# A Restormer block on one core: the depthwise conv of every fourth channel chunk on TensorE in 5 of 12 middle bands instead of 3 of 7, with the whole instruction order computed anew

## The chip, the cores and the metric

The kernel runs on one core of a Trainium2 chip. The metric is device time in microseconds (us). The engines are TensorE (PE, with its weight loads as PEld), VectorE (DVE), ScalarE (ACT), GpSimd (POOL) and SyncE (SP, which only issues DMAs here). The time before is 4030.19 us, the median of three runs.

## The reference

The input is 16 images of 128 channels by 96 by 96 pixels, all in float32. Each image goes through a block of two parts:

```python
xn1 = layernorm(x over channels)
q, k, v = xn1 @ wq.T, xn1 @ wk.T, xn1 @ wv.T       # 8 heads of 16 channels
attn = softmax((q / |q|) @ (k / |k|).T * 16**-0.5)  # 16 x 16 for each head, over all pixels
x = x + (attn @ v) @ wp.T
xn2 = layernorm(x over channels)
h1 = w_in @ xn2                                     # 128 -> 512 channels
h2 = depthwise 3x3 conv of h1, zero padding          # 9 taps for each channel
x = x + w_out @ gelu(h2)                            # 512 -> 128 channels
```

The attention is over channels, so one image's attention needs a sum over all its pixels before any pixel can go on. The feed-forward part is local to a pixel, but for the 3x3 conv.

## The kernel before

**Tiles.** An image is cut into 6 bands of 16 rows (`BR`), a band into 4 units of 4 rows (`UR`, 384 pixels). Over all images there are 96 bands, numbered g. The 512 hidden channels are 4 chunks n of 128. Normalised pixels lie in a ring of rows (`xn`), from which TensorE reads.

**Two ways to do a conv.** For chunks 0, 1 and 2 of each band, and for chunk 3 of some, the conv is a *job* (`conv_job`). TensorE computes the hidden rows (`hidden`, L952), 16 to 18 of them in three or four matmuls; a float32 matmul stands in the trace as two instructions. ScalarE moves each to SBUF with its bias (`kept`, L955). VectorE does six of the nine taps, plus the centre, as six `scalar_tensor_tensor` instructions on 16 rows (`tap`, L982): the first reads 1536 elements per partition, the others 1520, or 1425 where the outer tap row lies outside the image. For the other two taps ScalarE writes the product (`product`, L975) and GpSimd issues DMAs that add one product to the other and the sum to the result (`add_products`, L989: one is "add_last", one is "add_first"). ScalarE copies two rows to the top of the buffer for the next band (`halo`, L947) and applies gelu (L993).

For chunk 3 of the other bands (`by_matmuls`), TensorE does everything: each tap's diagonal is multiplied into the weights beforehand (`comp`), so that nine products accumulate in PSUM for each unit (L1047), and ScalarE applies gelu with the right bias at the image's edges (L1062, three instructions a unit, six where the unit touches the top or the bottom). There is no DVE tap, no product, no added DMA and no halo in that way.

Which bands go the second way is decided by `by_pe(g)`:

```python
k = NG - 1 - g
if g < NB:
    return g in PE_FIRST
return k in PE_LAST if k < NB else (k + 1) * PE_SHARE[0] // PE_SHARE[1] > k * PE_SHARE[0] // PE_SHARE[1]
```

The first image (bands 1, 3, 5) and the last (`PE_LAST`, four bands) have lists of their own; `PE_SHARE` holds for the 84 bands between.

**After the conv.** `ffn_out` multiplies the four chunks with `woutT` (L1082, eight instructions a unit), ScalarE copies the result (`evicted`, L1092), and a DMA issued by GpSimd adds a band to the output in DRAM (`add_out`, L1096), to which SP has stored the attention's result (`store_x2`). In the last two bands VectorE adds (L1089) and SP stores.

**Around it.** Each image has two norm passes: transposes to pixels (L694), statistics on VectorE (L701), the power on GpSimd (L712), scaling on ScalarE (L737), for the first pass the gram matrix (L746), transposes back (L780) and a copy into the ring (L783). The attention between them is a chain of small steps on all engines. `mix` (L643) applies it, ScalarE moves the result (`mixed`, L652), and a DMA issued by GpSimd adds the input (`add_x`, L655).

**The order.** Every step is put on record as an operation with an engine, a duration, a due place counted in jobs, and what it reads and writes. `Plan.order` plays all of them through once, when the kernel is built: an engine that is free takes the ready operation with the lowest place, if a buffer is free, and the operations are written out in the order of their starts. On the chip each engine then runs its own list in this order. A place is the job's number plus an offset from `AT`, with separate offsets (names ending in `_0`) for the first image; `SLACK` adds to how long a result is held back for other engines, and `add` and `move` set the durations of DMAs issued by GpSimd and SP:

```python
def add(p, f, r, w, n=BR, dram=False):
    late = T_DRAM if dram else (0, 0.01)
    op("POOL", 800, p, f, r, w, 350 + SLACK["ADD"], late[1], (T_ADD[0] + n * (T_ADD[1] + late[0])) * 108 / 100)
```

There are 15 buffers for results and products of the conv (`h3`), 4 PSUM banks shared by `hidden`, `by_matmuls`, `ffn_out` and `mix`, and two PSUM buffers for the transposes to pixels.

Of the kernel before, what the change touches and what calls it, by code (L numbers as in the profile page):

```python
# [19 lines left out]
XR = 8  # L20
RING = 124
PE_CHUNK = 3
PE_SHARE = [3, 7]
PE_LAST = (0, 1, 3, 4)
PE_FIRST = [1, 3, 5]
HEAD = 2
# [10 lines left out]
LAST_ADDS = 2  # L37
IN_TURN = ("tr", "xb", "x1")
AT = dict(
    load_1=-98.0, load_2=97.25, tables=85.15, weights=-792.45, zeros=79.7, load_a=-138.9, forth_a=-4.35,  # L40
    stats_a=-21.2, variance_a=-32.7, power_a=-106.65, scaled_a=-54.6, gram=7.8, back_a=-40.4, place_a=-40.15,
    attention=-134.7, mix=-2.85, residual=-281.65, mixed=-12.35, add_x=85.8, forth_b=-9.45, stats_b=-42.85,
    variance_b=31.9, power_b=-14.4, shift_b=-138.5, scaled_b=-461.4, back_b=-7.75, place_b=288.55, evicted=90.4,
    add_out=52.9, halo=120.1, hidden=4.7, kept=-885.75, products=643.55, add_last=35.65, tap=248.3,
    add_first=70.15, gelu=273.2, conv=3.75, conv_gelu=-926.85, out=8.15, add=-117.65, store=67.75, mix_0=-49.95,
    residual_0=-107.3, mixed_0=-51.7, add_x_0=25.0, gram_0=363.7, forth_a_0=-122.3, forth_b_0=-8.35,
    stats_a_0=6.3, stats_b_0=31.35, scaled_a_0=-127.55, scaled_b_0=120.9, back_a_0=-24.7, back_b_0=-58.05,
    place_a_0=-41.75, place_b_0=-85.55, shift_b_0=-22.25, late=69.2, store_x2=-58.9, store_x2_0=-116.55,
    variance_a_0=-270.4, variance_b_0=-83.0, power_a_0=-136.0, power_b_0=76.85, attention_0=-297.05,
    load_a_0=-428.55, hidden_0=2.8, kept_0=126.55, products_0=350.15, tap_0=79.7, add_last_0=-519.2,  # L50
    add_first_0=-230.95, gelu_0=18.6, conv_0=2.5, conv_gelu_0=113.55, out_0=6.35, evicted_0=-10.75,
)
STEP = dict(scaled=0.3, hidden=0.1, products=0.5, tap=0.166, conv=1.6, conv_tap=0.03, out=0.8, out_part=0.05)
SLACK = dict(PE=450, DVE=120, ACT=130, POOL=400, ADD=420, MOVE=290)
NORM1_END = 6.0
EARLY = 5
WAIT = dict(POOL=1130, SP=1470, ACT=1470)
# [4 lines left out]
T_ADD, T_DRAM, T_MOVE = (65, 227), (15, 750), 125  # L62


class Plan:
# [15 lines left out]
    def op(self, engine, ns, place, work, reads, writes, result, own=None, dma=0, two=False):  # L81

        k = len(self.ops)
        needs = {}
        for t in reads:
            if t in self.writer:  # L90
                needs[self.writer[t]] = True
        for t in writes:
            if t in self.writer:
                needs[self.writer[t]] = True
            for r in self.readers.get(t, ()):
                needs[r] = True
        for t in reads:
            self.readers.setdefault(t, []).append(k)
        new = []
        for t in writes:  # L100
            self.writer[t], self.readers[t] = k, []
            if t[0] in self.free and t[:2] not in self.users and t[:2] not in new:
                new.append(t[:2])
        for t in {t[:2]: None for t in (*reads, *writes)}:
            if t[0] in self.free:
                self.users.setdefault(t, []).append(k)
                needs[self.users[t][0]] = True
        needs.pop(k, None)
        self.ops.append((engine, ns, place, work, list(needs), new, result, own or result, dma, two))
# [129 lines left out]
def tile_restormer_block(  # L239
# [138 lines left out]
    op = plan.op  # L378
# [27 lines left out]
    def pe(ns, p, f, r, w):  # L406
        op("PE", ns, p, f, r, w, ns + 200 + SLACK["PE"], ns)

    def dve(ns, p, f, r, w, two=False):
        op("DVE", ns, p, f, r, w, ns + 120 + SLACK["DVE"], ns + 125, two=two)  # L410

    def pool(ns, p, f, r, w):
        op("POOL", ns, p, f, r, w, ns + 33 + SLACK["POOL"])

    def add(p, f, r, w, n=BR, dram=False):
        late = T_DRAM if dram else (0, 0.01)
        op("POOL", 800, p, f, r, w, 350 + SLACK["ADD"], late[1], (T_ADD[0] + n * (T_ADD[1] + late[0])) * 108 / 100)

    def move(p, f, r, w, n=XR):
        op("SP", 430, p, f, r, w, 350 + SLACK["MOVE"], dma=n * T_MOVE)  # L420

    def act(ns, p, f, r, w):
        op("ACT", ns, p, f, r, w, ns + 150 + SLACK["ACT"], ns + 144)

# [202 lines left out]
    def norm(i, second, place_of):  # L627
# [8 lines left out]
        def x2(s, u):  # L636
# [35 lines left out]
            if u % UPX == UPX - 1:  # L672
                add(at("add_x", s, i), add_x, [], whole, XR, True)
# [257 lines left out]
    def conv_job(j, g, n):  # L931
# [82 lines left out]
        for k, t in enumerate(dma_taps[1:]):  # L1014
            add(at("add_last", j, g >= HEAD), lambda t=t: add_products(t), [pr[1 + k]], [pr[0]], rows_of(t))
# [3 lines left out]
        if dma_taps:  # L1019
            add(at("add_first", j, g >= HEAD), lambda: add_products(dma_taps[0]), [pr[0]], h3, rows_of(dma_taps[0]))  # L1020
# [103 lines left out]
    def by_pe(g):  # L1124
# [5 lines that stand above are left out]
# [57 lines left out]
```

## Time and profile before

| | |
|---|---|
| median of three runs | 4030.19 us (4029.83 to 4032.23) |
| the profiled execution's own time | 4030.8 us |
| its span, first to last instruction | 4029.1 us |
| granted TensorE clock, mean | 0.999 |
| PE busy | 3983.6 us (99%) |
| PEld busy | 2602.8 us (65%) |
| DVE busy | 3959.4 us (98%) |
| ACT busy | 3707.7 us (92%) |
| POOL busy | 1889.7 us (47%) |

A group's row reads: line, engine, operation, result and operands, count, then busy time in us and mean ns of one, then the engine's idle time just before these instructions. Busy time counts overlapping instructions of one engine once. In a table of windows each engine's entry is its busy us, with the number of instructions in brackets, and behind them stand the granted clock, the mean busy share of the 16 DMA engines and GB/s.

### The profile page before, as it was taken

The page shows a single profiled execution, that of the slowest core. Times are in us where ns is not written, and L with a number is a line of the kernel's source. Part 1 is how long each engine was busy: PE and PEld are TensorE (multiplying, and loading weights), DVE is VectorE, ACT ScalarE, POOL GpSimd, SP SyncE. Part 2 cuts the span into 40 slices and gives each one's busy share as a digit, 9 for nine tenths or more (in the row PEclk, how much of TensorE's full clock was granted, in tenths as well). Part 3 has the DMA queues.
Part 4 walks back from the last instruction along what each step waited for, and adds up shares of the span by engine and source line. Part 5 has one row for each costly group of instructions (what it writes and reads, how often), then busy time and mean ns, then how long its engine had stood idle before and what let it go on. Part 6 is the DMA issues. An engine that isn't in the chain of part 4 may idle for free. (4 is left out here: it accounts for less than half of the span.)

```text
span 4029.1 us, 51274 instructions
## 1 busy us (share of the span) xinstructions
PE 3983.6 (99%) x17112; PEld 2602.8 (65%) x17112; DVE 3959.4 (98%) x3472; ACT 3707.7 (92%) x7680; POOL 1889.7 (47%) x1594
## 2 busy tenths in 40 slices
PE   9999999999999999999999999999999999999999
PEld 7666666666666666656666666666666666666565
DVE  6999999999999999999999999999999999999998
ACT  7999999899999999989989899999989999999985
POOL 4544455454454544545455453544545544454431
PEclk9999999999999999999999999999999999999999
DMA  5999899999999999999999999999999999999987
GB/s 147 208 197 223 185 214 205 209 225 197 220 222 201 218 203 230 213 202 219 198 216 210 198 220 198 230 205 211 224 194 227 206 217 216 202 221 189 218 177 152
DMA packets 196872, 832.64 MB, mean 207 GB/s; under 512 B 22784, under 2 KB 24320, under 8 KB 196608
## 3 DMA queue, kind: packets, MB, share of 16 engines
q0 software_dynamic: 138672, 677.52, 85.6%
q1 hardware_dynamic: 57936, 151.83, 10.5%
q8 instruction: 137, 2.24, 0.2%
q14 instruction: 127, 1.04, 0.1%
HBM read 150.62 MB, written 149.42 MB: 74 GB/s over the span
## 5 line engine op out<-in xcount | busy, mean ns | idle before, releaser
L982 DVE SCALAR_TENSOR_TENSOR h<-h,ratio,h 128x1520 f32<-128x1520 f32 (+1 forms) x1707 | 2980.5, 1780 | 8.0
L1082 PE MATMUL h<-h,woutT 128*128 128x384 f32 x3072 | 1135.3, 489 | 8.0 <-ACT h L955 7.1
L1047 PE MATMUL h<-xn,comp 128*128 128x380 f32 (+3 forms) x3162 | 1097.7, 476 | 1.8 <-ACT h L955 0.9
L975 ACT ACTIVATE h<-h,ratio 128x1536 f32<-128x1536 f32 (+1 forms) x680 | 1088.7, 1610 | 4.8 <-PE h L1082 2.9
L952 PE MATMUL h<-xn,winT 128*128 128x384 f32 (+3 forms) x2712 | 1059.9, 494 | 5.2 <-ACT h L955 2.2
L989 POOL DMA_DIRECT2D h<-h x680 | 640.2, 968 | 892.2 <-ACT h L975 390.1
L955 ACT ACTIVATE h<-h,beta 128x384 f32<-128x384 f32 (+1 forms) x1314 | 794.1, 632 | 83.0 <-PE h L952 67.6
L1082 PEld LDWEIGHTS h<-h,woutT 128*128 128x128 f32 x3072 | 557.6, 191 | 347.3 <-issue 39.9
L1047 PEld LDWEIGHTS h<-xn,comp 128*128 128x128 f32 x3162 | 567.0, 190 | 312.9 <-issue 16.6
L712 POOL TENSOR_TENSOR rstd_a<-ve_a,mhalf 128x4 f32<-128x4 f32 x288 | 508.8, 1767 | 449.4 <-ACT ve_a L708 429.0
L712 POOL TENSOR_TENSOR rstd_b<-ve_b,mhalf 128x4 f32<-128x4 f32 x288 | 537.1, 1886 | 351.6 <-ACT ve_b L708 337.9
L952 PEld LDWEIGHTS h<-xn,winT 128*128 128x128 f32 x2712 | 485.6, 190 | 276.1 <-issue 21.8
L982 DVE SCALAR_TENSOR_TENSOR h<-h,ratio 128x1536 f32<-128x1536 f32 x341 | 617.7, 1812 | 2.5 <-ACT h L955 1.4
L993 ACT ACTIVATE h<-h 128x1536 f32<-128x1536 f32 (+1 forms) x344 | 520.1, 1514 | 8.4 <-DMA h<-h 4.5
L737 ACT ACTIVATE zT<-pT_b,rstd_b 128x128 f32<-128x128 f32 x1132 | 331.5, 409 | 21.9 <-POOL rstd_b L712 20.7
L737 ACT ACTIVATE zT<-pT_a,rstd_a 128x128 f32<-128x128 f32 x1080 | 318.1, 412 | 3.2 <-POOL rstd_a L712 1.6
L746 PEld LDWEIGHTS g<-zT 128*128 128x128 f32 x2160 | 275.3, 191 | 43.2 <-issue 0.4
L643 PE MATMUL h<-xn,mwT 128*128 128x384 f32 x768 | 296.3, 489 | 3.5 <-ACT h L1062 1.0
L655 POOL DMA_DIRECT2D x<-in_x_dram x189 | 179.2, 964 | 238.4 <-ACT x L652 161.8
L746 PE MATMUL g<-zT 128*128 128x129 f32 x2160 | 285.2, 274 | 0.0
L652 ACT ACTIVATE x<-h,d 128x384 f32<-128x384 f32 x378 | 225.8, 629 | 13.0 <-PE h L643 7.2
L1062 ACT ACTIVATE h<-h,edge 128x376 f32<-128x376 f32 (+2 forms) x558 | 162.6, 387 | 71.2 <-PE h L1047 70.5
(185 smaller groups left out, 3212.6 us busy)
## 6 DMA issues: line engine op xcount, KB each, us to landing
h<-h POOLq DMA_DIRECT2D x567, 768.0 KB, 10.0
h<-h POOLq DMA_DIRECT2D x113, 720.0 KB, 11.9
x<-in_x_dram SPq DMA_DIRECT2D x192, 384.0 KB, 7.8
out_dram<-x SPq DMA_DIRECT2D x190, 384.0 KB, 9.6
x<-in_x_dram POOLq DMA_DIRECT2D x189, 384.0 KB, 10.3
out_dram<-h POOLq DMA_DIRECT2D x94, 768.0 KB, 10.4
out_dram<-x SPq DMA_DIRECT2D x4, 192.0 KB, 1.9
h<-in_L_conv_w_in_dram SPq DMA_DIRECT2D x1, 256.0 KB, 2.8
```

Source lines behind the costliest of these rows:

```text
L643: nc.tensor.matmul(rows(pm), lhsT=mats[i][0], rhs=interior(i, u), start=True, stop=True)
L712: nc.gpsimd.tensor_tensor(rstd, d["ve"], mhalf, ALU.pow)
L737: nc.scalar.activation(zT(q)[:, k, :P], d["pT", q][:, k, :], AF.Copy, scale=d["rstd"][:, t : t + 1])
L746: nc.tensor.matmul(grams[i][:, : P + 1], lhsT=zt[:, :P], rhs=zt, start=(q == 0 and k == 0), stop=(q == NU * TPU // QT - 1 and k == QT - 1),)
L952: nc.tensor.matmul(rows(ph)[:, k : k + m, :], lhsT=winT[:, n, :], rhs=z, start=True, stop=True)
L955: nc.scalar.activation(window(h1_, r, e - r, 1), rows(d.pop(("ph", r))), AF.Identity, bias=beta[:, n : n + 1])
L975: nc.scalar.activation(d["pr", t][:, o0:o1, :], shifted(t, o0, o1), AF.Copy, scale=ratio[:, n, t : t + 1])
L982: nc.vector.scalar_tensor_tensor(h3[:, o0:o1, w0:w1], shifted(t, o0, o1, w0, w1), ratio[:, n, t : t + 1], onto, ALU.mult, ALU.add)
L989: nc.gpsimd.dma_start(out=to[:, o0:o1, :], in_=d["pr", t][:, o0:o1, :], accum_op=ALU.add)
L993: nc.scalar.activation(h3, h3, AF.Gelu)
L1047: nc.tensor.matmul(d["pc"][:, o0 + k : o0 + k + m, w0:w1], lhsT=comp[:, t, :], rhs=z[:, :, w0 + dx : w1 + dx], start=(t == order[0]), stop ...
L1082: nc.tensor.matmul(rows(d["po"]), lhsT=woutT[:, n, :], rhs=h3s[g, n][:, s * UR : (s + 1) * UR, :], start=(k == 0), stop=(k == NCH - 1),)
```

## The change

`PE_SHARE` becomes 5 of 12. Of the 84 bands of the 14 middle images 35 instead of 36 have their fourth chunk on TensorE, and they lie at other places: with 5 of 12 the pattern repeats every two images. The offsets of all due places, two slacks and the planner's costs of an accumulating DMA are other numbers too, and the order that follows from them is computed anew. No instruction's own code changes.

```diff
-PE_SHARE = [3, 7]
+PE_SHARE = [5, 12]
...
 AT = dict(
-    load_1=-98.0, load_2=97.25, tables=85.15, weights=-792.45, zeros=79.7, load_a=-138.9, forth_a=-4.35,
-    stats_a=-21.2, variance_a=-32.7, power_a=-106.65, scaled_a=-54.6, gram=7.8, back_a=-40.4, place_a=-40.15,
-    attention=-134.7, mix=-2.85, residual=-281.65, mixed=-12.35, add_x=85.8, forth_b=-9.45, stats_b=-42.85,
-    variance_b=31.9, power_b=-14.4, shift_b=-138.5, scaled_b=-461.4, back_b=-7.75, place_b=288.55, evicted=90.4,
-    add_out=52.9, halo=120.1, hidden=4.7, kept=-885.75, products=643.55, add_last=35.65, tap=248.3,
-    add_first=70.15, gelu=273.2, conv=3.75, conv_gelu=-926.85, out=8.15, add=-117.65, store=67.75, mix_0=-49.95,
...
+    load_1=67.95, load_2=66.0, tables=-10.25, weights=-1.25, zeros=102.0, load_a=-138.05, forth_a=-4.35,
+    stats_a=-71.15, variance_a=-7.95, power_a=-38.85, scaled_a=-26.15, gram=7.8, back_a=-19.55, place_a=-53.7,
+    attention=-132.65, mix=-2.85, residual=-143.35, mixed=-11.45, add_x=583.2, forth_b=-9.45, stats_b=-240.2,
+    variance_b=3.45, power_b=-0.35, shift_b=62.8, scaled_b=-128.9, back_b=-8.05, place_b=116.65, evicted=28.7,
+    add_out=137.25, halo=51.0, hidden=4.7, kept=-219.85, products=688.85, add_last=163.15, tap=38.55,
+    add_first=429.0, gelu=66.75, conv=3.75, conv_gelu=-117.0, out=8.15, add=-143.05, store=-82.3, mix_0=-98.55,
...
 )
-SLACK = dict(PE=450, DVE=120, ACT=130, POOL=400, ADD=420, MOVE=290)
+SLACK = dict(PE=440, DVE=120, ACT=130, POOL=400, ADD=420, MOVE=0)
...
-        op("POOL", 800, p, f, r, w, 350 + SLACK["ADD"], late[1], (T_ADD[0] + n * (T_ADD[1] + late[0])) * 108 / 100)
+        op("POOL", 1000, p, f, r, w, 350 + SLACK["ADD"], late[1], (T_ADD[0] + n * (T_ADD[1] + late[0])) * 107 / 100)
```

The offsets cut here include `store_x2` (-58.9 before, -176.25 after) and all those of the first image.

More of the change, by code (lines that the diff above doesn't have):

```diff
@@ L45 @@
-    add_first=70.15, gelu=273.2, conv=3.75, conv_gelu=-926.85, out=8.15, add=-117.65, store=67.75, mix_0=-49.95,
[L46 to L49, printed above, removed]
@@ L50 @@
-    load_a_0=-428.55, hidden_0=2.8, kept_0=126.55, products_0=350.15, tap_0=79.7, add_last_0=-519.2,
-    add_first_0=-230.95, gelu_0=18.6, conv_0=2.5, conv_gelu_0=113.55, out_0=6.35, evicted_0=-10.75,
+    load_1=67.95, load_2=66.0, tables=-10.25, weights=-1.25, zeros=102.0, load_a=-138.05, forth_a=-4.35,
+    stats_a=-71.15, variance_a=-7.95, power_a=-38.85, scaled_a=-26.15, gram=7.8, back_a=-19.55, place_a=-53.7,
+    attention=-132.65, mix=-2.85, residual=-143.35, mixed=-11.45, add_x=583.2, forth_b=-9.45, stats_b=-240.2,
@@ new lines @@
+    variance_b=3.45, power_b=-0.35, shift_b=62.8, scaled_b=-128.9, back_b=-8.05, place_b=116.65, evicted=28.7,
+    add_out=137.25, halo=51.0, hidden=4.7, kept=-219.85, products=688.85, add_last=163.15, tap=38.55,
+    add_first=429.0, gelu=66.75, conv=3.75, conv_gelu=-117.0, out=8.15, add=-143.05, store=-82.3, mix_0=-98.55,
+    residual_0=102.75, mixed_0=-53.0, add_x_0=-59.8, gram_0=147.5, forth_a_0=134.55, forth_b_0=-7.8,
+    stats_a_0=-37.7, stats_b_0=-37.4, scaled_a_0=76.85, scaled_b_0=46.25, back_a_0=147.9, back_b_0=-39.95,
@@ L52 @@
+    place_a_0=123.9, place_b_0=-117.0, shift_b_0=-120.65, late=153.0, store_x2=-176.25, store_x2_0=-117.5,
+    variance_a_0=75.05, variance_b_0=-414.1, power_a_0=-184.2, power_b_0=188.85, attention_0=-138.6,
+    load_a_0=-265.85, hidden_0=2.7, kept_0=2.25, products_0=120.45, tap_0=3.0, add_last_0=-99.45,
+    add_first_0=157.4, gelu_0=11.85, conv_0=2.4, conv_gelu_0=74.5, out_0=7.35, evicted_0=65.7,
 )
 STEP = dict(scaled=0.3, hidden=0.1, products=0.5, tap=0.166, conv=1.6, conv_tap=0.03, out=0.8, out_part=0.05)
-SLACK = dict(PE=450, DVE=120, ACT=130, POOL=400, ADD=420, MOVE=290)
+SLACK = dict(PE=440, DVE=120, ACT=130, POOL=400, ADD=420, MOVE=0)
```

## The prediction

> **What bounds the kernel now.** I read the busy times first, then a table of three windows (head, middle, tail), then the groups by shape, the chain of waits, VectorE's waits in the middle, and the order of time at the end.
>
> ```profile
> PE 3983.6 (99%) x17112; PEld 2602.8 (65%) x17112; DVE 3959.4 (98%) x3472; ACT 3707.7 (92%) x7680; POOL 1889.7 (47%) x1594
> ```
> ```profile
> 0.00:100.00 100.00, 90.99 (x556) 71.19 (x557) 65.70 (x158) 73.14 (x214) 47.29 (x79) 1.00 0.55 146
> 100.00:3950.00 3850.00, 3817.09 (x16328) 2487.84 (x16327) 3827.63 (x3271) 3596.47 (x7407) 1832.02 (x1504) 1.00 0.98 210
> 3950.00:4030.00 80.00, 75.53 (x232) 43.72 (x231) 66.04 (x45) 38.12 (x61) 10.39 (x12) 0.99 0.65 137
> ```
>
> By the first row PE is the fullest engine, with DVE one percent behind. The windows turn that round: in the 3850 us of the middle DVE is idle for 3850 - 3827.6 = 22.4 us, PE for 32.9. DVE's other idle time lies in the head (34.3 us) and the tail. PE's number also flatters PE, as the rows of its long groups and two pieces of the chain show:
>
> ```profile
> L1082 PE MATMUL h<-h,woutT 128*128 128x384 f32 x3072 | 1135.3, 489 | 8.0 <-ACT h L955 7.1 <-ACT h L993 0.8
> ```
> ```profile
> 3443.07 2.58 PE h L952 x8
> 3540.92 2.56 PE h L1047 x8
> ```
>
> One matmul of 384 columns lasts 489 ns, but eight in a row take 2.58 us, 322 ns each: each overlaps its successor by a third, and a pause of up to 167 ns behind one still counts as busy. The Trainium skill, Perfetto Trace Analysis, Identifying the Most-Contended Engine, says the same as a rule: matmul busy time does not tell how full TensorE is, the share of weight loads does, and for VectorE the busy share is fair; the engine found fullest is the one to relieve. By that rule (PEld 65%, DVE 98%) the change would load the wrong engine. The rows agree as to the order of the two, though 65% is too low here: 322 ns for each matmul leaves no such room.
>
> So DVE paces the middle, narrowly, and PE is close behind. DVE's waits in the middle are few:
>
> ```profile
> DVE st_b L701 <- PE pT_b L694: 6.1, 12, 1.2
> DVE st_a L701 <- PE pT_a L694: 1.2, 4, 0.5
> DVE h L982 <- ACT h L955: 1.1, 3, 0.5
> DVE h L982 <- PE h L1082: 0.8, 3, 0.3
> DVE n L875 <- PE g L869: 0.6, 3, 0.3
> ```
>
> PE is named for 8.7 us (6.1 + 1.2 + 0.8 + 0.6) of the 22.4.
>
> **How many bands.** With k from 6 to 89, `by_pe` picks 38 - 2 = 36 bands by 3 of 7 and 37 - 2 = 35 by 5 of 12. With the three of the first image and the four of the last it is 43 before and 42 after, so 341 jobs become 342. Listing the bands from the formula, those at an image's top go from 6 to 7, those at its bottom from 8 to 2. At these a job's two outer taps are short, so the change in shapes is more than one job's worth.
>
> **Taken from TensorE.** A full band's conv is 4 units of 9 products: 4 x (3 x 384 + 6 x 380) = 13728 columns; a band at an image's edge has 286 fewer. Bands at edges fall from 14 to 9, so PE loses 13728 - 5 x 286 = 12298 columns. At 322 ns for 384 columns and two instructions a product (1.677 ns a column) that is 20.6 us. The hidden rows come back: the same listing gives 1824 columns more for `hidden` (one job more, three halos fewer), 3.1 us. PE's net change is -17.5 us.
>
> **Added to VectorE.** The rows by shape:
>
> ```profile
> L982 DVE SCALAR_TENSOR_TENSOR h<-h,ratio,h 128x1520 f32<-128x1520 f32 x1477 | 2606.4, 1793 | 7.2
> L982 DVE SCALAR_TENSOR_TENSOR h<-h,ratio 128x1536 f32<-128x1536 f32 x341 | 617.7, 1812 | 2.5 <-ACT h L955 1.4 <-PE h L1082 0.8
> L982 DVE SCALAR_TENSOR_TENSOR h<-h,ratio,h 128x1425 f32<-128x1425 f32 x228 | 384.1, 1695 | 0.6
> ```
>
> Taps overlap a little too, so the cost of one is busy time by count: 1.765, 1.811 and 1.685 us. One job more gives one more of 1536; five more jobs at tops and bottoms (one fewer, six more) with two short taps each give ten more of 1425; the rest of six taps is five fewer of 1520. The sum is 1.811 + 16.85 - 8.82 = 9.8 us on DVE. Nothing hides it in the middle, where DVE is 99.4% busy; its cover would have to be the 22.4 us of idle time.
>
> **ScalarE, GpSimd and DMA.**
>
> ```profile
> L975 ACT ACTIVATE h<-h,ratio 128x1536 f32<-128x1536 f32 (+1 forms) x680 | 1088.7, 1610 | 4.8 <-PE h L1082 2.9
> L955 ACT ACTIVATE h<-h,beta 128x384 f32<-128x384 f32 (+1 forms) x1314 | 794.1, 632 | 83.0 <-PE h L952 67.6 <-DVE h L982 7.9
> L993 ACT ACTIVATE h<-h 128x1536 f32<-128x1536 f32 (+1 forms) x344 | 520.1, 1514 | 8.4 <-DMA h<-h 4.5 <-DVE h L982 3.7
> L1062 ACT ACTIVATE h<-h,edge 128x376 f32<-128x376 f32 (+2 forms) x558 | 162.6, 387 | 71.2 <-PE h L1047 70.5
> L947 ACT COPY h<-h 128x192 f32<-128x192 f32 x250 | 100.0, 400 | 0.0
> L989 POOL DMA_DIRECT2D h<-h x680 | 640.2, 968 | 892.2 <-ACT h L975 390.1 <-DVE h L982 262.4 <-ACT zT L737 38.3
> ```
> ```profile
> q0 software_dynamic: 138672, 677.52, 85.6%
> h<-h POOLq DMA_DIRECT2D x567, 768.0 KB, 10.0
> h<-h POOLq DMA_DIRECT2D x113, 720.0 KB, 11.9
> ```
>
> ACT gains two products (3.2 us) and a gelu (1.5) and loses 27 edge gelus (3 x 4 of the band, 15 at edges; 7.9), three halos (1.2) and one `kept` (0.6): -5.0 us, on an engine idle 8% of the time. POOL issues two more DMAs, 1.9 us of an engine that is idle for half; no cost. The DMA engines are another matter, busy 0.98 in the middle. Adds go to 682, of which 118 of 720 KB: 1.3 MB more. At 85.6% of 4029.1 us for 677.5 MB (5.09 us a MB) that is 6.6 us of all sixteen. Below the 9.8 us of DVE, this doesn't set the end while adds land in about 10 us and the 15 buffers cover them; it costs up to 6.6 us, beside DVE's, where they don't.
>
> **The new order.** On PE the offsets of `hidden`, `conv`, `out`, `mix`, `forth` and `gram` in the middle are the same numbers. On ACT, which takes the lowest place first, `kept` and `conv_gelu` still come ahead of nearly all and `products` last. On DVE statistics stay ahead of taps. On POOL the two norms' powers stay first, but `add_last`, then first of the DMAs, goes behind `add_out`, and `add_first` (70.15, now 429.0) and `add_x` (85.8, now 583.2) go far behind both. Each of those issues takes 0.97 us on POOL, so one that is passed by a band's `add_out` or a sum comes about 1 us later, against landing in 10; behind it wait gelu (ACT), then `out` (PE), then the buffer. On SP `store_x2` goes ahead of `load_a`, which has a place 138 jobs early in both and is bound by buffers. I price the order at 0, with bounds of -22.4 us (all DVE idle time of the middle gone) and +20.6 us (rival three). DVE's waits on PE may shrink, as PE has 17.5 us more room: between 0 and 8.7 us; I take 1.5, because the transposes that they wait for are themselves held up by ACT and POOL, which the change doesn't relieve:
>
> ```profile
>   issue: 34.1, 180
>   POOL rstd_b L712: 20.7, 24
>   ACT zT L737: 10.9, 15
>   PE pT_b L694: 6.1, 12
> ```
>
> (These are the idle times of the engines ahead of instructions on `pT_b`, by what ended them.) In the head the two weight loads change places and the first image's offsets are all new; bounds are DVE's 34.3 us of idle time there and as much on the other side if it doubled, but the first image's bands and work are the same, so I take 0.
>
> **The tail.**
>
> ```profile
> 4007.31 18.22 PE L1082 MATMUL h<-h,woutT 128*128 128x384 f32 x56
> ```
> ```profile
> 4012.53 3.14 ACT L993 ACTIVATE h<-h 128x384 f32<-128x384 f32 x5 [3.69 <-DVE h L982]
> ```
>
> DVE's last tap releases the last gelu at 4012.5, and PE still works off `out` to 4025.5: 13.0 us. PE is behind at the end. Were it not, the last chunk's eight matmuls and the pieces of gelu would take about 5.7 us (2.58 + 3.14), 7.3 less. The last image's bands are the same four, so PE is as full there as before; I take 0 of the 7.3.
>
> **The sum**, against the profiled execution's own 4030.8 us (span 4029.1 and 1.7 around it): 4030.8 + 9.8 - 1.5 = 4039.1. That execution stands 0.6 above the median of the runs, so the forecast is 4038.5 us, with 4032 to 4046 as its own range (all of the 8.7 us taken back, or all of DMA's 6.6 paid).
>
> **Rivals.**
>
> *One: PE paces.* For it speaks PE's 99% and that PE ends last; against it, DVE's 99.4% in the middle. PE alone would give 4030.2 - 17.5 = 4012.7, but DVE must then fit in, and with all 22.4 us of its idle time gone it reaches 4030.2 + 9.8 - 22.4 = 4017.6. So 4018 us: faster. It decides if DVE's idle time in the middle falls below 22.4 - 9.8 - 8.1 = 4.5 us.
>
> *Two: the two share the pace.* The tail gives its 7.3 us, and half of the waits on PE go (4.4): 4030.2 + 9.8 - 11.7 = 4028 us, no change that can be told.
>
> *Three: the late sums.* With `add_first` last on POOL and DMA at 0.98, results complete later, the 15 buffers run out, and taps or products wait for one. What a bad stretch looks like:
>
> ```profile
> 500.00:600.00 100.00, 96.59 (x386) 60.12 (x385) 97.95 (x85) 93.33 (x191) 49.80 (x43) 1.00 0.97 207
> ```
>
> DVE is idle for 2.05 us there against 22.4 / 38.5 = 0.58 on average. One such stretch more in each of the 14 middle images gives 14 x 1.47 = 20.6 us: 4059 us. Against it: in the whole trace DVE's taps wait for no DMA.
>
> That the change doesn't do what it says is excluded by the count of bands.
>
> **How the numbers follow.** About 0.2% (8 us, 4022 to 4038) is what a measurement can tell from no change. Chances: forecast 0.48, rival one 0.20, two 0.15, three 0.17. The forecast straddles the limit of slower: I give 0.27 of it to slower and 0.21 to the same. Rival three is slower; of rival two 0.13 is the same and 0.02 faster. Faster 0.22, same 0.34, slower 0.44. The range, 4017 to 4060, reaches from rival one's floor to rival three; what lies outside is half of each of the two, below 0.2.
>
> **What would show it.** Right: 342 openings of 1536 and 238 of 1425 on L982, L1047's columns down, DVE busy up by about 10 us, its idle time in the middle still near 20, PE's idle time there up from 33 towards 50, the tail behind the last tap still 13 us. Rival one: DVE idle in the middle below 5 us. Two: the tail near 6 us. Three: taps or ACT's products that wait for a DMA or a gelu, and DVE idle above 40 us. I am wrong altogether if DVE's busy time rises by much less than 9.8 us, or if the head changes by more than a few us.

## The result and the profile after

The kernel after takes 4024.85 us against 4032.36 us before (medians of twelve runs each), a ratio of 0.9982 with a 95% interval of 0.9973 to 0.9990. It is 7.5 us faster, a little under the 0.2% that the prediction took as its limit. The forecast was 8 us slower; the sign was wrong, the range held the time. The profiled execution took 4024.71 us with a span of 4023.0.

The busy times and the three windows of after, to be read against those of before:

```profile
PE 3970.2 (99%) x17024; PEld 2580.7 (64%) x17024; DVE 3958.9 (98%) x3478; ACT 3695.3 (92%) x7652; POOL 1918.9 (48%) x1596
```
```profile
0.00:100.00 100.00, 90.45 (x551) 70.75 (x552) 64.94 (x156) 72.69 (x209) 42.44 (x78) 1.00 0.52 142
100.00:3950.00 3850.00, 3810.28 (x16263) 2469.83 (x16262) 3832.06 (x3282) 3589.17 (x7390) 1868.64 (x1510) 1.00 0.98 210
3950.00:4030.00 80.00, 69.46 (x214) 40.14 (x212) 61.89 (x42) 33.47 (x55) 7.81 (x9) 0.99 0.62 130
```

VectorE's busy time did not rise by 10 us; it fell by 0.5. Its idle time in the middle fell from 22.4 to 17.9 us, TensorE's rose from 32.9 to 39.7. The groups of VectorE's taps by shape, and the DMA issues, have the counts that the prediction gave:

```profile
L982 DVE SCALAR_TENSOR_TENSOR h<-h,ratio,h 128x1520 f32<-128x1520 f32 x1472 | 2589.1, 1790 | 4.3
L982 DVE SCALAR_TENSOR_TENSOR h<-h,ratio 128x1536 f32<-128x1536 f32 x342 | 618.6, 1810 | 2.0 <-ACT h L955 1.9
L982 DVE SCALAR_TENSOR_TENSOR h<-h,ratio,h 128x1425 f32<-128x1425 f32 x238 | 400.2, 1692 | 0.6
```
```profile
q0 software_dynamic: 138960, 678.85, 85.7%
h<-h POOLq DMA_DIRECT2D x564, 768.0 KB, 10.0
h<-h POOLq DMA_DIRECT2D x118, 720.0 KB, 13.5
```

At the end, the last gelu on ScalarE is released 3.3 us earlier than before, and TensorE still works off `out`, now for 10.2 us (from 4009.22 to 4019.45) where it was 13.0:

```profile
4001.23 18.22 PE L1082 MATMUL h<-h,woutT 128*128 128x384 f32 x56
```
```profile
4009.22 1.76 ACT L993 ACTIVATE h<-h 128x384 f32<-128x384 f32 x4 [2.01 <-DVE h L982]
```

**Two accounts.** Where did VectorE's 10 us go? Two taps on the same result are a chain: the second reads what the first writes. In the trace of before a tap of 1520 elements is followed by the next instruction's start after 1.712 us, but after 1.830 if that is a tap on the same result. A recorded tap lasts 1.793 us on average, so some 80 of these 118 ns count as busy; the rest is a gap of 36 ns, too short for the lists of waits. Of the 22.4 us of VectorE's idle time in the middle of before, 7.7 are such gaps. With the order of instructions beside the trace they can be counted: 224 such pairs before, 139 after. The table splits the span of a profile for each engine into work (its instructions at their usual spacing; of VectorE's, the taps alone are listed), pairs, and all the rest, which is waiting; the middle is 100 to 3950 us of the span. All numbers but the ratios are us, worked out from the starts in each trace; ratios are those of the timed runs. The kernels below the first two are those of the next section.

| kernel | ratio to before | span | taps | pairs | VectorE waits, middle | TensorE work | TensorE waits, middle |
|---|---|---|---|---|---|---|---|
| before | 1 | 4029.1 | 3487.7 | 25.6 | 19.4 | 3930.3 | 77.1 |
| after | 0.9982 | 4023.0 | 3497.0 | 15.7 | 15.1 | 3912.3 | 89.4 |
| share_alone | 1.0013 | 4042.6 | 3497.0 | 27.9 | 23.1 | 3912.4 | 107.9 |
| order_alone | 0.9991 | 4027.0 | 3487.7 | 22.5 | 19.3 | 3930.2 | 75.3 |
| before_pe_less | 0.9953 | 4023.7 | 3487.7 | 25.4 | 13.4 | 3907.4 | 94.6 |
| before_dve_less | 0.9972 | 4026.8 | 3467.4 | 24.8 | 39.8 | 3930.2 | 76.4 |
| share_dve_less | 1.0014 | 4041.4 | 3485.0 | 27.2 | 35.5 | 3912.5 | 108.5 |
| after_pe_less | 0.9968 | 4016.4 | 3497.0 | 15.7 | 8.7 | 3890.2 | 105.1 |
| after_dve_less | 0.9951 | 4020.9 | 3476.7 | 15.8 | 32.8 | 3911.7 | 87.5 |

From before to after VectorE's account reads: taps +9.3, pairs -9.9, waits in the middle -4.3, head +1.8, from the last tap to the end -2.8; sum -5.9 of the span's -6.1. TensorE's reads: work -18.0, waits in the middle +12.3. Both are true at once, and neither says by itself which engine made the time.

### The profile page after: what moved, and what is told of

The parts are those of the page before. It is cut to its first block, busy times and chain, and to the rows that moved or that the text cites. A ratio compares the mean times of both kernels' runs of the same rounds, so it can differ in the third digit from the quotient of the medians.

```text
span 4023.0 us, 51123 instructions
## 1 busy us (share of the span) xinstructions
PE 3970.2 (99%) x17024; PEld 2580.7 (64%) x17024; DVE 3958.9 (98%) x3478; ACT 3695.3 (92%) x7652; POOL 1918.9 (48%) x1596
## 5 line engine op out<-in xcount | busy, mean ns | idle before, releaser
L1047 PE MATMUL h<-xn,comp 128*128 128x380 f32 (+4 forms) x3078 | 1079.0, 478 | 3.5 <-ACT xn L783 1.9
L952 PE MATMUL h<-xn,winT 128*128 128x384 f32 (+2 forms) x2708 | 1067.6, 495 | 7.9 <-ACT h L955 4.5
L955 ACT ACTIVATE h<-h,beta 128x384 f32<-128x384 f32 (+1 forms) x1313 | 805.7, 649 | 89.0 <-PE h L952 75.0
L1047 PEld LDWEIGHTS h<-xn,comp 128*128 128x128 f32 x3078 | 551.0, 190 | 304.1 <-issue 17.3
L712 POOL TENSOR_TENSOR rstd_b<-ve_b,mhalf 128x4 f32<-128x4 f32 x288 | 551.6, 1923 | 341.8 <-ACT ve_b L708 337.5
L737 ACT ACTIVATE zT<-pT_b,rstd_b 128x128 f32<-128x128 f32 x1132 | 334.8, 421 | 19.2 <-POOL rstd_b L712 17.9
L783 ACT COPY xn<-pB_a 128x384 f32<-128x384 f32 x384 | 199.2, 519 | 19.8 <-PE pB_a L780 17.6
```

The lines of the kernel that those rows point to most:

```text
L712: nc.gpsimd.tensor_tensor(rstd, d["ve"], mhalf, ALU.pow)
L737: nc.scalar.activation(zT(q)[:, k, :P], d["pT", q][:, k, :], AF.Copy, scale=d["rstd"][:, t : t + 1])
L952: nc.tensor.matmul(rows(ph)[:, k : k + m, :], lhsT=winT[:, n, :], rhs=z, start=True, stop=True)
L955: nc.scalar.activation(window(h1_, r, e - r, 1), rows(d.pop(("ph", r))), AF.Identity, bias=beta[:, n : n + 1])
L1047: nc.tensor.matmul(d["pc"][:, o0 + k : o0 + k + m, w0:w1], lhsT=comp[:, t, :], rhs=z[:, :, w0 + dx : w1 + dx], start=(t == order[0]), stop ...
```

## The experiments

Each ratio is to the kernel before, run on the same chip, in five rounds. The kernel after was timed only beside before in the set above. Before's median was 4032.36 us there and 4032 to 4041 us in the five sets here, so where a kernel is set against after, two ratios to before are compared, and a shift of up to 0.2% from set to set may hide in that.

**The two halves of the change.** The share alone, and all the rest alone:

```diff
 # share_alone, from before             # order_alone, from after
-PE_SHARE = [3, 7]                      -PE_SHARE = [5, 12]
+PE_SHARE = [5, 12]                     +PE_SHARE = [3, 7]
```

> The kernel before with only the share changed to 5 of 12; offsets, slacks and costs stay those of before. In its order 244 taps of VectorE directly follow a tap on the same result (before 224, after 139); in the traces such a tap starts about 115 ns later than one that follows other work. Theory 1 (VectorE paces, and the order pays by fewer of such pairs): 9.2 us more of taps and 20 x 0.115 = 2.3 us of pairs, so 11 us slower than before, ratio 1.003. Theory 2 (TensorE paces, and its 17.5 us less pay): 8 to 17 us faster, ratio 0.996 to 0.998.

> The kernel after with only the share set back to 3 of 7; offsets, slacks and costs are those of after. 198 dependent pairs of taps against 224 before. Theory 1: 26 x 0.115 = 3 us faster than before, ratio 0.999, with up to 3 us of noise of the order. Theory 2: as before, ratio 1.000, since TensorE's work is that of before.

Measured: share_alone 1.0013 (1.0004 to 1.0022), order_alone 0.9991 (0.9978 to 1.0004). The share by itself makes the kernel slower by some 5 us, so theory 2, as it stood, is out, and theory 1's 1.003 lies outside the interval too; the rest by itself may save 4 us, which its interval doesn't separate from nothing. The table shows why the share alone doesn't pay: TensorE is rid of its 18 us there too, but waits 31 us more. Its waits for other engines in the middle, in before (two of its rows) and in share_alone:

```profile
PE pT_b L694 <- ACT zT L737: 3.1, 3, 2.6
PE pT_a L694 <- ACT zT L737: 1.6, 2, 1.1
```
```profile
PE pT_a L694 <- ACT zT L737: 9.6, 10, 2.2
PE pT_b L694 <- ACT zT L737: 7.5, 9, 1.9
PE h L643 <- ACT h L955: 4.8, 7, 1.6
```

and in after:

```profile
PE pT_a L694 <- ACT zT L737: 5.9, 3, 4.6
PE pT_b L694 <- ACT zT L737: 5.4, 9, 1.5
PE h L1082 <- ACT h L955: 4.9, 6, 1.5
```

TensorE waits for ScalarE to empty PSUM, and with before's offsets at the new share more often: the waits that the lists put down to ScalarE add up to 30.3 us (48 times) in before, 50.2 (75) in share_alone and 37.5 (62) in after.

**What a pair costs.** The planner's `own` time, after which VectorE may use its own result, decides whether other work is put between two taps:

```diff
 # pairs_many, from after; in pairs_few_before, from before, + 300
-        op("DVE", ns, p, f, r, w, ns + 120 + SLACK["DVE"], ns + 125, two=two)
+        op("DVE", ns, p, f, r, w, ns + 120 + SLACK["DVE"], ns, two=two)
```

> The kernel after, but the planner takes a VectorE result to be ready for VectorE at once instead of 125 ns later, so that it no longer puts other work between two taps on one result: 1223 dependent pairs instead of 139, the same instructions otherwise. Theory 1 (each pair costs the pace 115 ns): 1084 x 0.115 = 125 us slower than after, 4150 us, ratio to before 1.029. Theory 2 (TensorE paces and VectorE has room): less than a third of that, below 4070 us, ratio below 1.010.

> The kernel before (share 3 of 7, its offsets), but the planner takes a VectorE result to be ready for VectorE only 300 ns later: 165 dependent pairs instead of 224, the same instructions otherwise. Theory 1: 59 x 0.115 = 6.8 us faster than before, ratio 0.998. Theory 2: no change, ratio 1.000.

Measured: pairs_many 1.0296 (1.0280 to 1.0313), the 125 us that were expected. In order of time, VectorE in pairs_many: the tap at 1304.50 is followed by one on its own result 1.85 us later.

```profile
1304.50 1.81 DVE L982 SCALAR_TENSOR_TENSOR h<-h,ratio 128x1536 f32<-128x1536 f32 x1
1306.35 1.80 DVE L982 SCALAR_TENSOR_TENSOR h<-h,ratio,h 128x1520 f32<-128x1520 f32 x1
```

In after, the instruction of the same shape at 1308.98 is followed by a tap on another result 1.73 us later:

```profile
1308.98 1.81 DVE L982 SCALAR_TENSOR_TENSOR h<-h,ratio 128x1536 f32<-128x1536 f32 x1
1310.71 1.70 DVE L982 SCALAR_TENSOR_TENSOR h<-h,ratio,h 128x1425 f32<-128x1425 f32 x1
```

So a thousand pairs do set the pace; that eighty do isn't shown by this. For pairs_few_before missed: 1.0020 (1.0010 to 1.0030), slower, with 7 us less in pairs and 24 us more of VectorE's waits in the middle. With 300 ns told for 125, the planner made another order, and its waits cost more than the pairs that it saved.

**Pairs moved by hand.** Four kernels keep the planner's order and swap neighbours in VectorE's list (a tap with statistics, then a tap with a tap) where that changes the number of pairs and nothing in between depends on it, until the wanted number is reached:

```diff
-        return [ops[k][3] for k in sorted(range(len(ops)), key=lambda k: (starts[k], k))]
+        return [ops[k][3] for k in paired(self, sorted(range(len(ops)), key=lambda k: (starts[k], k)), 139)]
```

> The kernel before, its order kept but for swaps of two neighbours in VectorE's list, made until 139 taps instead of 224 directly follow a tap on the same result (the count of after). Theory 1 (VectorE paces, a pair costs 0.115 us): 85 x 0.115 = 9.8 us faster than before, ratio 0.9976. Theory 3 (two limits: at 3 of 7 TensorE paces as well, so that room on VectorE isn't used): no more than 3 us, ratio above 0.9992.

> Offsets, slacks and costs of after with the share 3 of 7, and neighbours swapped in VectorE's list until 139 pairs are left of 198: against after it differs in the share at an equal number of pairs. Theory 1: 9.2 us less of taps than after, so ratio to before 0.996, faster than after. Theory 3: TensorE's 17.5 us more take that back, ratio 0.998 to 1.000, no faster than after.

> The kernel after with neighbours swapped in VectorE's list until no more swap helps: 55 pairs instead of 139. Theory 1: 84 x 0.115 = 9.7 us faster than after, ratio to before 0.9958. Theory 3: the same as far as TensorE lets it; half of it or more, ratio below 0.997.

> The kernel after with neighbours swapped in VectorE's list the other way, until 224 pairs stand there, the count of before. Theories 1 and 3: 85 x 0.115 = 9.8 us slower than after, ratio to before 1.0006. Rival 2 (TensorE's 17.5 us less are what made it faster): as after, ratio 0.9982.

Measured: before_139 1.0060 (1.0048 to 1.0073), order_139 1.0031 (1.0019 to 1.0042), after_55 1.0024 (1.0015 to 1.0034), after_224 1.0068 (1.0055 to 1.0080). All four are slower than the kernels that they were made from (for order_139 that is order_alone), whichever way the pairs went, so by themselves they say nothing for or against the theories; they show what a swap costs otherwise. One difference fits the price of a pair: after_55 and after_224, the same list swapped in the two directions, lie 0.0044 apart, 18 us for 169 pairs, where 169 x 0.115 is 19. As the swaps are not the same ones, that is no proof. In the profiled execution of before_139, the slowest of its five, VectorE saves 9.9 us in pairs and waits 44 us more in the middle. The three longest of its waits there, which in before were 1.1, 6.1 and 1.2 us:

```profile
DVE h L982 <- ACT h L955: 16.3, 16, 2.7
DVE st_b L701 <- PE pT_b L694: 8.0, 16, 0.9
DVE st_a L701 <- PE pT_a L694: 5.0, 9, 0.9
```

A tap or a statistic that is moved by one place comes later for somebody, and the lists of the other engines are not moved with it.

**Which engine paces before.** Here work is added to or taken from one engine in the unchanged order:

```diff
 # before_pe_less: one product of a unit left out
-            for k, m, z in got:
+            for k, m, z in got if not (t == 7 and s == 1 and NB <= g < NG - NB) else ():
 # before_pe_more, after_pe_more: the first product twice (the call, cut here, stands in this loop)
+                for twice in (True, False) if t == order[0] and s == 1 and NB <= g < NG - NB else (False,):
 # before_dve_less: one tap left out in 12 jobs
-            nc.vector.scalar_tensor_tensor(
+            if not (t == 2 and n == 0 and NB <= g < NG - NB and g % 7 == 3): nc.vector.scalar_tensor_tensor(
```

> The kernel before with one of the nine conv products (the tap below the centre) left out in one unit of each of the 36 middle bands that TensorE does; so part of the conv is missing. Order and all other work as before. TensorE has 36 x 0.644 = 23.2 us less, more than the change takes. Theory 1 (VectorE paces): at most 4 us faster (the share of VectorE's waits on TensorE and of the tail), ratio above 0.999. Rival 2 (TensorE paces): 17 to 23 us faster, ratio 0.9943 to 0.9958. Theory 3 (both pace in turns): 6 to 12 us, ratio 0.997 to 0.9985.

> The kernel before with the first conv product done twice in one unit of each of the 36 middle bands that TensorE does (the second overwrites the first). TensorE has 23.2 us more, all else as before. Theory 1: at most 8 us slower, as TensorE is idle for 33 us in the middle, ratio below 1.002. Rival 2: 17 to 23 us slower, ratio 1.0043 to 1.0058. Theory 3: 9 to 16 us, ratio 1.002 to 1.004.

> The kernel after with the first conv product done twice in one unit of each of its 35 middle bands on TensorE: 22.5 us more on TensorE, which gives back all that the change took from it and 5 us; VectorE's list, with 139 pairs, as after. Theory 1: at most 6 us slower than after, still at or below before, ratio to before 0.998 to 0.9997. Rival 2: 17 to 22 us slower than after, ratio 1.0025 to 1.0037.

> The kernel before with one of the six taps left out in 12 of the jobs of the middle images; so part of the conv is missing. VectorE has 12 x 1.712 + 6 pairs x 0.118 = 21 us less, TensorE all that it had. Theory 1: 17 to 21 us faster, ratio 0.9948 to 0.9958. Rival 2: at most 3 us, ratio above 0.9992. Theory 3: 6 to 14 us, ratio 0.9965 to 0.9985.

Measured: before_pe_less 0.9953 (0.9937 to 0.9969), 19 us faster for 23.2 us less on TensorE; before_pe_more 1.0034 (1.0022 to 1.0045), 14 us slower for 23.2 us more; before_dve_less 0.9972 (0.9962 to 0.9983), 11 us faster for 21 us less on VectorE; after_pe_more 1.0004 (0.9992 to 1.0015): with the 18 us given back and 5 more, the gain of the change is gone. Theory 1 falls: it allowed 4 us for before_pe_less. That run came out where rival 2, TensorE alone, had put it; the two others came out as theory 3 had them. So before is held by both engines, and TensorE counts for at least as much; the two slopes (0.8 and 0.5) have intervals that overlap. Before's own runs spread here from 4029 to 4049 us, and part of both gains is that these kernels spread less. At the same mean clock of 0.998 the medians are 4030.9 us for before (nine runs), 4020.5 for before_pe_less (four) and 4028.5 for before_dve_less (eleven): 10 us for TensorE's 23, but only 2 for VectorE's 21. The clock is itself an outcome, so this is a reading and not a test, but it puts more on TensorE, and the profiled executions say the same. In the profiled execution of before_dve_less, which ran 2.3 us shorter than that of before, the 21 us have turned into waits:

```profile
100.00:3950.00 3850.00, 3819.83 (x16321) 2489.04 (x16320) 3810.06 (x3261) 3598.58 (x7409) 1817.58 (x1504) 1.00 0.98 210
```
```profile
DVE st_b L701 <- PE pT_b L694: 10.5, 18, 2.0
DVE st_a L701 <- PE pT_a L694: 5.9, 11, 1.1
DVE h L982 <- ACT h L955: 4.1, 4, 1.4
```

VectorE is idle for 39.9 us of the middle, 17.5 more than before, and its longest waits are for TensorE's transposes: 16.4 us against 7.3. An engine that was busy for 99.4% could not use the time that it was given in this execution.

**Which engine paces after, and TensorE's relief alone.**

```diff
 # share_dve_less, from share_alone: one tap left out in 7 jobs, so VectorE's list is as long as before
+            if not (t == 2 and n == 0 and NB <= g < NG - NB and g % 12 == 3): nc.vector.scalar_tensor_tensor(
 # after_dve_more: the first tap twice in 12 jobs
+            for _ in range(2 if t == left[0] and n == 0 and NB <= g < NG - NB and g % 7 == 3 else 1):
```

after_pe_less and after_dve_less are made from after as their namesakes were from before.

> The kernel before with the share 5 of 12 and its own offsets, and one tap left out in 7 of the jobs (part of the conv is missing): 12 us of taps away, so that VectorE's list, pairs included, is as long as before within 1 us, while TensorE has its 17.5 us less. Theory 4 (TensorE paces the kernel before, VectorE is close behind): 7 to 14 us faster than before, ratio 0.9965 to 0.9983. Theory 1 (VectorE paces): within 3 us of before, ratio above 0.9993.

> The kernel after with the first tap done twice in 12 of the jobs of the middle images (the second writes the same values again): 12 x 1.73 + 12 pairs x 0.118 = 22 us more on VectorE. Theory 4, if VectorE is at its limit in after: 10 to 20 us slower than after, ratio to before 1.0007 to 1.003. If TensorE paces after as it does before: at most 6 us slower than after, ratio to before below 0.9997.

> The kernel after with one conv product left out in one unit of each of its 35 middle bands on TensorE (part of the conv is missing): 22.5 us less on TensorE. If VectorE has taken over the pace in after: at most 6 us faster than after, ratio to before 0.9967 to 0.9982. If TensorE still paces: 10 to 20 us faster, ratio 0.993 to 0.9957.

> The kernel after with one tap left out in 12 jobs (part of the conv is missing): 20.6 us less on VectorE. If VectorE has taken over the pace in after: 10 to 20 us faster, ratio to before 0.993 to 0.9957. If TensorE still paces: at most 6 us faster than after, ratio 0.9967 to 0.9982, and VectorE's waits grow by what it was spared.

Measured against before: after_dve_more 1.0015 (1.0003 to 1.0026), after_pe_less 0.9968 (0.9956 to 0.9980), after_dve_less 0.9951 (0.9934 to 0.9967). Against after's 0.9982 that is 13 us slower for 22 more on VectorE, 6 faster for 22.5 less on TensorE, 12 faster for 20.6 less on VectorE. With after_pe_more (9 us slower for 22.5 more) the slopes are near 0.6 for VectorE and 0.25 to 0.4 for TensorE. Without after's own time, from less work to more: 26 us for 43 on VectorE (0.6, in one set), and 15 us for 45 on TensorE (0.3, in two sets where before's medians were 4039.16 and 4040.63); in before, 33 us for 46 on TensorE (0.7, in one set). After leans on VectorE where before leaned on TensorE; each difference by itself is within the errors, all together point one way. The chain of waits moved too. Its first line, before and after:

```profile
PE 18%; ACT 1%; DVE 1%; issue 0%; POOL 0%; POOLq 0%; DVEq 0%; ACTq 0%
```
```profile
PE 26%; DVE 10%; ACT 4%; issue 1%; DMA 1%; POOL 1%; POOLq 0%; DVEq 0%; ACTq 0%; SPq 0%
```

These are shares of the span, and each chain covers only the stretch over which it can be followed back from the end: 798 us in before, 1782 in after. Over the last 700 us, which both cover, TensorE holds 612 us of the chain in before and VectorE 22; in after it is 365 and 215. The order alone does not move it (order_alone 632 and 30); the share does (share_alone 312 and 287), and so does less work on TensorE in before's own order (before_pe_less 403 and 228).

share_dve_less is the miss that matters: 1.0014 (1.0005 to 1.0024). TensorE has 18 us less than before, VectorE no more, and the kernel is slower than before, just as slow as share_alone. By the table the 12 us that VectorE was spared became waits (23.1 to 35.5). With before's offsets at this share, VectorE's amount of work doesn't set the time, and TensorE's 18 us less didn't shorten it. What is left is the order in which the engines wait for each other; no run shows it by itself.

**What of the order.**

```diff
 # old_dma_cost, from after
-        op("POOL", 1000, p, f, r, w, 350 + SLACK["ADD"], late[1], (T_ADD[0] + n * (T_ADD[1] + late[0])) * 107 / 100)
+        op("POOL", 800, p, f, r, w, 350 + SLACK["ADD"], late[1], (T_ADD[0] + n * (T_ADD[1] + late[0])) * 108 / 100)
```

old_first_image sets `load_1`, `load_2`, `tables`, `weights`, `zeros`, `late` and all offsets ending in `_0` back to those of before.

> The kernel after, but the planner plays an accumulating DMA with the costs of before (800 ns of issue for 1000, 108/100 for 107/100); share, offsets and slacks are those of after, and no instruction differs, only their order. In the order that comes out 242 taps directly follow one on the same result instead of 139. If the gain hangs on an order that was found for just these numbers: pairs 103 x 0.118 = 12 us more on VectorE, of which it passes on some 0.6, and more waits on TensorE; 8 to 20 us slower than after, ratio to before 1.000 to 1.003. If offsets and share carry it: as after, ratio 0.997 to 0.9992.

> The kernel after with the offsets of the first image and of the weights set back to those of before; 136 pairs, the middle images planned by after's numbers. If the gain lies in the middle images: within 4 us of after, ratio to before 0.9972 to 0.999. If the first image's new offsets carry part of it: at least 5 us slower than after, ratio above 0.9994.

Measured: old_dma_cost 1.0025 (1.0016 to 1.0033), 17 us slower than after; old_first_image 0.9986 (0.9975 to 0.9997), no difference from after that can be told. In old_dma_cost no instruction and no offset differs from after. The planner merely thinks of a DMA's issue as 0.2 us shorter and of its transfer as 1% longer, and the order that follows has 242 pairs (27.6 us for 15.7), 12.8 us more of VectorE's waits in the middle and 24 us more of TensorE's.

## Why the prediction was wrong

**"DVE paces the middle."** This step failed. VectorE's 22.4 us of idle time were taken as proof that it sets the time and TensorE's 32.9 as room. before_pe_less (19 us for 23.2) and before_dve_less (11 us for 21) show that less work on either helps, on TensorE at least as much. Each engine runs a fixed list, and an engine that is a little late makes the other wait a little later. A sign of it was there and was read past: the chain of waits of before is TensorE's for 18 of 20 parts, though it covers no more than the last fifth of the span.

**TensorE's 17.5 us counted at nothing.** TensorE's work fell by 18.0 us, as worked out, but its worth did not follow from it. In before's order a us less on TensorE is worth about 0.8 (0.45 at equal clocks), yet with the bands at new places and the old offsets (share_alone) nothing was left of it; in after's order, giving it back costs the whole gain (after_pe_more).

**VectorE's 9.8 us.** The count and the size were right (9.3 by spacing). "Nothing hides it" was wrong: 9.9 us of pairs went at the same time. The prediction took busy time as work; the 25.6 us of pairs, two thirds of them in the busy time, could have been found in the starts of the taps.

**"I price the order at 0, with bounds of -22.4 and +20.6 us."** The value failed and the bounds held. Between share_alone and after, which do the same work, lie 0.0031 of the ratio, 12.5 us, measured in two sets.

**The small terms.** DVE's waits on PE fell by 1.8 us (8.7 to 6.9), where 1.5 was taken: this term held. The tail gave 2.8 of the 7.3 us where 0 was taken; profiles at the new share made here have 14.8 to 17.0 us from the last tap's start to the end, those at the old one 17.6 to 19.2. DMA's 1.3 MB and the 682 adds came as counted, and no DMA became the limit. The head cost VectorE 1.8 us in this profile; old_first_image shows no effect on the time.

**The rivals.** Rival two, both engines sharing the pace, was nearest: 4028 us, and its mechanism is the one that the runs bear out for before. Its terms were off: the tail gave 2.8 us for its 7.3, VectorE's waits in the middle 4.3 in all, of which those on PE 1.8 for its 4.4, and it left the pairs out.

**The range** held by what it had kept for the rivals: 4024.85 us lies below the forecast's own 4032 to 4046. So it is no support for the sum.

What stays open: how the 7 us divide between TensorE's relief and the fewer pairs, since the order can't be held while the share changes; and what an order searched for as long at 3 of 7, with as few pairs, would give. It wasn't tried.

## What to carry to other kernels

Two engines at 99% with fixed lists can pace together: before saying which one is the limit, take 20 us of work from each in turn, and see whether it comes off the time or turns into waits. Busy time can hold stalls where recorded durations overlap; compare the starts of instructions that depend on each other with those that don't. Where the order is planned for one set of numbers, a change of the amount of work may be worth little until the order is found anew; here 1% and 0.2 us in the planner's idea of a DMA cost 17 us, about as much as the work that was taken from TensorE.

## What the runs showed of the hardware

TensorE's granted clock can fall to half after pauses of some 2 us. In before, two pauses of 2.1 and 2.5 us for ScalarE lie between 2047.5 and 2053.5 us. Three windows of 3.41 us there, the first just ahead of the drop:

```profile
2047.93:2051.34 3.41, 1.01 (x8) 0.75 (x7) 3.41 (x3) 3.41 (x5) 0.00 (x0) 1.00 1.05 210
2051.34:2054.75 3.41, 1.28 (x2) 0.83 (x3) 3.41 (x3) 3.40 (x7) 1.79 (x2) 0.50 1.04 226
2054.75:2058.17 3.42, 3.42 (x7) 1.74 (x6) 3.42 (x4) 2.13 (x4) 1.04 (x1) 0.50 1.08 240
```

TensorE was busy for 1.01 of the 3.41 us ahead of the drop; the clock was then at half for 6.83 us, and came back after a window in which TensorE was busy throughout. The Trainium skill, TensorE: Matmul & The Clock Gate, Part 1, says that the clock is halved after an idle window of about 3.4 us and comes back after as much activity. The halving, the length of the window and the time to come back agree; the longest pause here was shorter than the window, so low activity was enough. That holds beyond this place: of 62 halvings in the middles of the traces made here, one followed 3.41 us without any matmul; the median had TensorE busy for 1.36 of them.

The drops go with a run's time: of 29 runs of before on one chip, those with a mean clock of 0.998 took 4029 to 4039 us, those with 0.996 took 4048. The twelve runs of after have 0.999 to 1.000. Whether the drops cost the time or only mark the stalls that do was not separated: after_pe_more had no drop in its middle and took 4038.02 us.
